# The feed-forward layernorm of a sequence's two halves, taken together in one PSUM bank

## The chip, the cores and the metric

One core of a Trainium2 chip runs the whole kernel. The time is the device time of one execution in microseconds, and a kernel's time is the median of its runs.

The engines are named as in the profile: PE (TensorE matmuls), PEld (TensorE weight loads), DVE (VectorE), ACT (ScalarE), POOL (GpSimd), SP (SyncE, which issues most DMAs).

## The reference, cut to what matters

`x` is (32 sequences, 256 tokens, 256 features). A state-space block (projection, causal convolution of 4 taps, layernorm, a scan over the 256 tokens, gate, projection) gives the input of two transformer layers. The result is added to `x`. The change is in the second half of a layer, the feed-forward:

```python
def _layer(x, wqkv, qs, ksc, wo, lg, lb, w1, b1, w2, b2):
    ...                                  # attention; x = x + o @ wo
    h = shift_token(x)                   # the second 128 features come from the token before
    mu = h.mean(-1, keepdims=True)
    var = h.var(-1, keepdims=True)
    h = (h - mu) / jnp.sqrt(var + 1e-05) * lg + lb
    h = h @ w1 + b1                      # 256 -> 2 x 682
    a, g = jnp.split(h, 2, axis=-1)
    h = a * jax.nn.gelu(g, approximate=False)
    x = x + h @ w2 + b2
    return x
```

All data are float32.

## The kernel before, in words

**Layout.** The 32 sequences make 4 groups of 8. In the transformer a sequence's state is `res[b]`, features in the partitions (two blocks of 128, `KM`) and tokens along the row. [...] PE transposes a half of the sequence (`W` = 128 tokens, `NW` = 2 halves) into a PSUM bank, DVE takes mean and variance per token, POOL raises variance plus epsilon to the power -1/2, DVE normalises, PE transposes back, and ACT copies to `hT` with gain and bias.

**Two streams.** The scan of the state-space block is a chain of 1024 DVE steps (L703, `h`), each on a row that a DMA spreads over the partitions (`xrep`) and ACT scales (L693). The first group's scan runs alone. The scans of groups 2 to 4 run beside the attention and feed-forward of the group before, which are 64 passes in all (4 groups, 2 layers, 8 sequences). The last group's layers run alone.

**Order.** Work is written as stages: `stage(n, i, what)` puts a piece into slot `8 * n + i`, where `n` counts the 64 passes. A loop walks through the slots and advances the scan by two steps in each slot, so 16 scan steps go with one pass, and a chunk of the scan (32 steps) with two. Within that order a scheduler may shift instructions of one engine against another engine's when the program is built, so an engine's final order isn't quite that of the slots. Instructions in `keep_in_program_order` keep their place on their engine. [...]

**PSUM.** All of it is one pool, `ps_w`, of 8 banks of 128 x 512 float32 under one tag. Each `bank(...)` takes a bank that was given back, in turn, so a new tile usually waits for the last reader of the tile of some seven allocations before.

**Pieces around the change**, with slots counted from the pass's slot 0 of the feed-forward:

- `Attention.sums` (slot 7 of the pass before): the softmax sums, then `rinv` on DVE (L1195). `values`: `ov` in two banks, each copied by ACT to oT (L1213).
- `turn` (slot 0, and slot 6): 8 transposes `tr_qk` (L1001) of a rotated query and key, copied by ACT to qT and kT (L1006).
- `project` (slots 0, 1, 1 and 3, 4, 4): `project_qkv` makes value, query and key of a half in one bank each (`ps_qkv`, L962); `rotated` reads query and key with ACT (`sq`, L975) and DVE (`rot` L978, `swp` L983), then POOL (L986, L994, L995).
- `FeedForward.normalise(w)` (slots 0 and 1 for the halves 0 and 1): two transposes `tp_h` (L1248), `st` (L1252), `mv` (L1254), `ve` (L1256), the power `rstd` (L1258). `apply(w)` (slots 1 and 2): `hn` (L1265). `spread(w)` (slots 2 and 3): two transposes `tp_hn` (L1278) and two ACT copies to `hT` (L1280).
- `scores` (slots 2, 3, 5): `sc` in two banks each, mask and products (L1161, L1168), exponentials to pT (L1177).
- `widen(m)` (slots 4 to 9): `pa` (L1301), the gelu of its half on ACT (`ag`, L1309). `product(m)` (a slot later): DVE multiplies into `ag` (L1317), which frees the bank of `pa`. The sixth chunk has only 42 rows (682 = 5 x 128 + 42) and is multiplied twice. So the last `widen` and `product` of one pass lie beside the layernorm of the next.
- `narrow(d)` (slots 3 and 4 of the next pass): `po_f` (L1329), added to `res` or `fo` by DVE (L1340).

Of the kernel before, what the change touches and what calls it, by code (L numbers as in the profile page):

```python
# [10 lines left out]
FP = mybir.dt.float32  # L11
# [3 lines left out]
ALU = mybir.AluOpType  # L15
# [4 lines left out]
P = 128  # L20
S = 256
DM = 256
KM = DM // P
# [15 lines left out]
W = 128  # L39
NW = S // W  # L40
# [3 lines left out]
LN_EPS = 1e-5  # L44
# [29 lines left out]
def kernel(  # L74
# [29 lines left out]
    nc = tc.nc  # L104
# [40 lines left out]
    ident = const.tile([P, P], FP, tag="ident", name="ident")  # L145
# [24 lines left out]
    neg_half = const.tile([P, HEADS], FP, tag="neg_half", name="neg_half")  # L170
# [43 lines left out]
    for i in range(2):  # L214
        t = const.tile([P, NI * (P + GB)], FP, tag=f"ly{i}", name=f"ly{i}")
# [3 lines left out]
    def program(ctx, exact):  # L219
# [7 lines left out]
        ap_ = ctx.enter_context(tc.tile_pool(name="at", bufs=2, reuse_waits="tile"))  # L227
        aw = ctx.enter_context(tc.tile_pool(name="aw", bufs=3, reuse_waits="tile"))
        ps_w = ctx.enter_context(tc.tile_pool(name="psw", bufs=8, space=PSUM, reuse_waits="tile"))

        def bank(pool, tag, name):
            return pool.tile([P, DI], FP, tag=tag, name=name)
# [681 lines left out]
        def scan_slots(groups):  # L914


            slots, scans = {}, [group_scan(g) for g in groups]
            for part in range(2):
                for i, agendas in enumerate(scans):
                    for s, what in agendas[part].items():  # L920
                        slots.setdefault(i * S + s, []).extend(what)
            for s in range(min(slots), max(slots) + 1):
                for what in slots.get(s, ()):
                    what()
                yield s


        ys, res, wt, projected = {}, {}, {}, {}

        def load_res(g, b):  # L930
            t = rpool.tile([P, KM, 1 + S], FP, tag=f"res{b}", name=f"res{b}")
            nc.gpsimd.memset(t[:, :, 0:1], 0.0)
            nc.sync.dma_start(out=t[:, :, 1:], in_=ys[g][:, :, b, :])
            res[b] = t

        def load_weights(l, kind, i=0):
            shape, srcs = {
                "qkv": lambda: ([P, KM, DI], [wqkv[:, l, :, i * DI : (i + 1) * DI]]),
                "wo": lambda: ([P, NC_, DM], [wo[:, l]]),
                "w1": lambda: (  # L940
                    [P, KM, 2, MCH[i][1]],
                    [w1[:, l, :, x * HID + MCH[i][0] :][:, :, 0 : MCH[i][1]] for x in range(2)],
                ),
                "w2": lambda: ([P, len(MCH), DM], [w2[:, l]]),
            }[kind]()
            t = wpool.tile(shape, FP, tag=f"{kind}{i}", name=f"{kind}{i}")
            for x, src in enumerate(srcs):
                nc.sync.dma_start(out=t[:, :, x] if len(srcs) > 1 else t, in_=src)
            if kind == "w2":
                last = len(MCH) - 1  # L950
                nc.sync.dma_start(out=t[DH : DH + MREM, last], in_=w2[0:MREM, l, last])
            wt[kind, i] = t
# [174 lines left out]
        class Attention:  # L1127
# [3 lines left out]
            def __init__(self, l):  # L1131
                self.l = l
                self.qkv, self.rot, self.p, self.o = {}, {}, {}, {}
# [102 lines left out]
        class FeedForward:  # L1236
# [2 lines left out]

            def __init__(self, g, l, b):  # L1240
                self.g, self.l, self.b = g, l, b
                self.hn, self.pa, self.ag = {}, {}, {}

            def normalise(self, w):
                tp = bank(ps_w, "w", "tp_h")
                for k in range(KM):
                    t0 = 1 - k + w * W
                    nc.tensor.transpose(  # L1248
                        tp[:, k * P : (k + 1) * P], res[self.b][:, k, t0 : t0 + W], ident
                    )  # L1250
                st = aw.tile([P, 6], FP, tag="st", name="st")
                nc.vector.bn_stats(st, tp[:, 0:DM])  # L1252
                mv = aw.tile([P, 2], FP, tag="mv", name="mv")
                nc.vector.bn_aggr(mv, st)  # L1254
                ve = aw.tile([P, 1], FP, tag="ve", name="ve")
                nc.vector.tensor_scalar_add(ve, mv[:, 1:2], LN_EPS)  # L1256
                rstd = aw.tile([P, 1], FP, tag="rstd", name="rstd")
                nc.gpsimd.tensor_tensor(rstd, ve, neg_half[:, 0:1], ALU.pow)  # L1258
                self.hn[w] = tp, mv, rstd

            def apply(self, w):
                tp, mv, rstd = self.hn[w]
                hn = ap_.tile([P, DM], FP, tag="hn", name="hn")
                tc.keep_in_program_order(
                    nc.vector.tensor_scalar(  # L1265
                        hn, tp[:, 0:DM], mv[:, 0:1], rstd, ALU.subtract, ALU.mult
                    )
                )
                self.hn[w] = hn

            def spread(self, w):
                if w == 0:
                    self.h = ap_.tile([P, KM, S], FP, tag="hT", name="hT", bufs=1)
                hn = self.hn.pop(w)
                tp = bank(ps_w, "w", "tp_hn")
                for k in range(KM):
                    ks = slice(k * P, (k + 1) * P)
                    nc.tensor.transpose(tp[:, ks], hn[:, ks], ident)  # L1278
                for k in range(KM):
                    nc.scalar.activation(  # L1280
                        self.h[:, k, w * W : (w + 1) * W],
                        tp[:, k * P : (k + 1) * P],
                        AF.Identity,
                        bias=flb_sb[:, self.l, k : k + 1],
                        scale=flg_sb[:, self.l, k : k + 1],
                    )
# [65 lines left out]
        if exact:  # L1352
            for g in range(NG):
                for _ in scan_slots([g]):
                    pass
                for b in range(GB):
                    load_res(g, b)
                for l in range(L):
                    for kind, i in WEIGHTS:
                        load_weights(l, kind, i)  # L1360
                    for _ in attention(l):
                        pass
                    for b in range(GB):
                        ff = FeedForward(g, l, b)
                        for w in range(NW):
                            ff.normalise(w)
                            ff.apply(w)
                            ff.spread(w)
                        for m in range(NM):
                            ff.widen(m)  # L1370
                            ff.product(m)
                        for d in range(KM):
                            ff.narrow(d)
            return
# [8 lines left out]
        def stage(n, i, what, *args):  # L1383
            stages.setdefault(ST * n + i, []).append(partial(what, *args))
# [18 lines left out]

        def feed(n, g, l, b):
            ff = FeedForward(g, l, b)
            for w in range(NW):
                stage(n + 1, 8 + w, ff.normalise, w)
                stage(n + 2, 1 + w, ff.apply, w)
                stage(n + 2, 2 + w, ff.spread, w)
            for m in range(NM):  # L1410
                stage(n + 2, 4 + m, ff.widen, m)
                stage(n + 2, 5 + m, ff.product, m)
            for d in range(KM):
                stage(n + 3, 3 + d, ff.narrow, d)
# [16 lines left out]
        for n, (g, l, b) in enumerate(seqs):  # L1431
            nxt = (ats[n + 1], seqs[n + 1][2]) if n + 1 < len(seqs) else None
            attend(n, ats[n], b, nxt)
            feed(n, g, l, b)
# [39 lines left out]
    with tc.If(fits > 0) as which:  # L1474
        with ExitStack() as es:
            program(es, False)
    with which.Else():
        with ExitStack() as es:
            program(es, True)
# [108 lines left out]
```

## Time and profile before

| | us |
|---|---|
| median of 3 runs (3755.57 to 3771.47) | 3759.6 |
| the profiled execution: its time | 3750.8 |
| the profiled execution: its span | 3748.7 |
| 600 to 2850 us, layers and scans together: PE busy, of 2250 | 2186.0 |
| 2850 to 3750 us, layers alone: PE busy, of 900 | 887.9 |

| instruction of the layernorm | count | mean ns |
|---|---|---|
| `st`, DVE L1252 | 128 | 427 |
| `mv`, DVE L1254 | 128 | 176 |
| `ve`, DVE L1256 | 128 | 149 |
| `rstd`, POOL L1258 | 128 | 646 |
| `hn`, DVE L1265 | 128 | 542 |
| `hT`, ACT L1280 | 256 | 453 |

The profile is of one execution. [...] The times in the waits view are those in which the waiting engine stood still; what released it is inferred. [...]

### The profile page before, as it was taken

The page shows a single profiled execution, that of the slowest core. Times are in us where ns is not written, and L with a number is a line of the kernel's source. Part 1 is how long each engine was busy: PE and PEld are TensorE (multiplying, and loading weights), DVE is VectorE, ACT ScalarE, POOL GpSimd, SP SyncE. Part 2 cuts the span into 40 slices and gives each one's busy share as a digit, 9 for nine tenths or more (in the row PEclk, how much of TensorE's full clock was granted, in tenths as well). Part 3 has the DMA queues.
Part 4 walks back from the last instruction along what each step waited for, and adds up shares of the span by engine and source line. Part 5 has one row for each costly group of instructions (what it writes and reads, how often), then busy time and mean ns, then how long its engine had stood idle before and what let it go on. Part 6 is the DMA issues. An engine that isn't in the chain of part 4 may idle for free.

```text
span 3748.7 us, 57254 instructions
## 1 busy us (share of the span) xinstructions
PE 3601.1 (96%) x19900; PEld 2242.4 (60%) x19900; DVE 2669.6 (71%) x5177; ACT 2195.4 (59%) x3817; POOL 1834.9 (49%) x1776
## 2 busy tenths in 40 slices
PE   7999889999999999999999999999999999999998
PEld 4444335656656665665666665656666666666666
DVE  6888889888787787778777877777777444444443
ACT  4666656666666666666666665666666444444442
POOL 4433466545555565455455555645444444434441
PEclk9999999999999999999999999999999999999999
DMA  7777655445454545434444545444443211011101
GB/s 210 205 198 202 189 163 149 120 117 135 127 137 129 147 123 146 120 112 122 120 128 116 147 124 147 121 108 126 112 129 103 57 40 50 12 34 34 30 25 35
DMA packets 469214, 435.81 MB, mean 116 GB/s; under 512 B 228835, under 2 KB 308532, under 8 KB 468788
## 3 DMA queue, kind: packets, MB, share of 16 engines
q1 hardware_dynamic: 384466, 420.05, 40.1%
q10 hardware_dynamic: 84450, 12.01, 2.0%
q8 instruction: 160, 2.62, 0.3%
q14 instruction: 138, 1.13, 0.1%
HBM read 383.70 MB, written 46.66 MB: 115 GB/s over the span
## 4 chain that ended last, share of the span: by engine, by line
PE 62%; DVE 16%; POOL 7%; ACT 6%; DMA 5%; issue 3%; SPq 0%; ACTq 0%; DVEq 0%; POOLq 0%
PE ps_qkv L962 12%; PE pa L1301 12%; PE po_f L1329 7%; DVE h L703 6%; PE y L715 4%; PE ps_wo L1012 4%; DMA xrep<-xnd 4%; PE sc L1168 4%; PE ov L1206 3%; PE ps_out L793 2%; ACT xrep L693 2%; DVE acc L485 2%; PE tr_qk L1001 2%; PE ps_in L395 2%; POOL acc L474 2%
## 5 line engine op out<-in xcount | busy, mean ns | idle before, releaser
L703 DVE CUSTOM_DVE_ANT_0 h<-h,xrep,lim 128x512 f32<-128x512 f32 x1024 | 948.2, 926 | 269.2 <-ACT xrep L693 238.8
L693 ACT ACTIVATE xrep<-xrep,beta 128x512 f32<-128x512 f32 x960 | 674.1, 719 | 333.0 <-DMA xrep<-xnd 235.9
L962 PE MATMUL ps_qkv<-qkv,res 128*128 128x512 f32 x1536 | 727.1, 610 | 45.2 <-DVE ag L1317 30.1
L1301 PE MATMUL pa<-hT,w 128*128 128x256 f32 (+1 forms) x3072 | 688.3, 386 | 0.3 <-ACT oT L1213 0.3
L1301 PEld LDWEIGHTS pa<-hT,w 128*128 128x128 f32 (+1 forms) x3072 | 492.9, 178 | 183.7 <-issue 66.5
L962 PEld LDWEIGHTS ps_qkv<-qkv,res 128*128 128x128 f32 x1536 | 282.4, 194 | 335.4 <-issue 263.3
L986 POOL TENSOR_TENSOR rot<-rot,swp 128x512 f32<-128x512 f32 x256 | 336.5, 1314 | 293.0 <-DVE swp L983 239.2
L1258 POOL TENSOR_TENSOR rstd<-ve,neg_half 128x1 f32<-128x1 f32 x128 | 82.7, 646 | 792.9 <-DVE ve L1256 787.8
L994 POOL TENSOR_TENSOR rn<-ss,neg_half 128x8 f32<-128x8 f32 x256 | 460.3, 1798 | 14.8 <-DVE ss L992 5.0
L1329 PE MATMUL po_f<-ag,w 128*128 128x256 f32 (+1 forms) x1536 | 387.8, 394 | 4.8 <-DVE res L1340 1.1
L715 PE MATMUL y<-h,ly 128*32 128x512 f32 x2048 | 354.9, 612 | 12.9 <-DVE h L703 11.7
L1329 PEld LDWEIGHTS po_f<-ag,w 128*128 128x128 f32 (+1 forms) x1536 | 273.6, 190 | 112.9 <-issue 44.6
L1317 DVE SCALAR_TENSOR_TENSOR ag<-pa,b_sb,ag 128x256 f32<-128x256 f32 (+1 forms) x448 | 212.4, 474 | 166.5 <-ACT ag L1309 163.0
L975 ACT ACTIVATE sq<-ps_qkv 128x512 f32<-128x512 f32 x256 | 152.1, 596 | 270.5 <-PE ps_qkv L962 234.6
L995 POOL TENSOR_TENSOR rot<-rot,rn 128x512 f32<-128x512 f32 x256 | 298.6, 1166 | 20.1
L1309 ACT ACTIVATE ag<-pa,b_sb 128x256 f32<-128x256 f32 x320 | 150.4, 470 | 198.5 <-PE pa L1301 197.4
L1012 PE MATMUL ps_wo<-oT,wo 128*128 128x256 f32 x1024 | 231.6, 379 | 0.0
L485 DVE SCALAR_TENSOR_TENSOR acc<-xr,wc_sb,acc 128x256 f32<-128x256 f32 x384 | 192.7, 525 | 52.9 <-POOL acc L474 52.6
L1177 ACT ACTIVATE pT<-sc 128x512 f32<-128x512 f32 x384 | 208.5, 596 | 32.2 <-PE sc L1168 30.7
L1168 PE MATMUL sc<-qT,kT 64*128 64x128 f32 (+1 forms) x2048 | 221.5, 345 | 0.0
L978 DVE TENSOR_TENSOR rot<-ps_qkv,rc_sb 128x512 f32<-128x512 f32 x256 | 175.0, 683 | 56.5 <-ACT sq L975 55.9
L1012 PEld LDWEIGHTS ps_wo<-oT,wo 128*128 128x128 f32 x1024 | 194.5, 190 | 27.2 <-PE y L715 0.8
(150 smaller groups left out, 5534.7 us busy)
## 6 DMA issues: line engine op xcount, KB each, us to landing
xrep<-xnd SPq DMA_DIRECT2D x960, 256.0 KB
rb<-inv SPq DMA_DIRECT2D x128, 256.0 KB
xnd<-xn SPq DMA_DIRECT2D x64, 256.0 KB
qkv<-in_wqkv_dram SPq DMA_DIRECT2D x24, 512.0 KB
ahead<-xs_a SPq DMA_DIRECT2D x48, 256.0 KB
xp<-ahead SPq DMA_DIRECT2D x48, 256.0 KB
xd<-xnd SPq DMA_DIRECT2D x192, 64.0 KB
w<-in_w_dram SPq DMA_DIRECT2D x80, 128.0 KB
```

What stands on the lines that cost most here:

```text
L485: nc.vector.scalar_tensor_tensor(acc, xr[:, :, k : k + CH], wc_sb[:, ch, k : k + 1], acc, ALU.mult, ALU.add,)
L693: scaled = nc.scalar.activation(bx, ck[c].pop(("bx", t), bx), AF.Copy, scale=ck[c]["beta"][:, t : t + 1])
L703: nc.vector._custom_dve(TENSOR_ADD_SAT, out=h_new, in0=state["h"], in1=bx, s0=ck[c]["lim"][:, 0, t : t + 1], s1=ck[c]["lim"][:, 1, t : t + 1],
L715: nc.tensor.matmul(ck[c]["y", hb][32 * q : 32 * q + 32, :], ly[hb % 2][:, 32 * t : 32 * t + 32], ck[c].pop(("h", hb * TB + t)), start=(i = ...
L962: nc.tensor.matmul(ps, res[b][:, k, t0 : t0 + W], wt["qkv", a][:, k], start=(k == 0), stop=(k == KM - 1),)
L986: nc.gpsimd.tensor_add(rot, rot, swp)
L994: nc.gpsimd.tensor_tensor(rn, ss, neg_half, ALU.pow)
L995: nc.gpsimd.tensor_mul(rot, rot, bc(rn, 2, DH))
L1012: nc.tensor.matmul(po[:, d], wt["wo", 0][:, c, d * P : (d + 1) * P], oT[:, c, :], start=(c == 0), stop=(c == NC_ - 1),)
L1168: nc.tensor.matmul(banks[r][:, i, :], kT[rows, i0 + i, kw * W : (kw + 1) * W], qT[rows, i0 + i, kw * W :], start=False, stop=(i == n - 1),)
L1301: nc.tensor.matmul(pg if x else pa, wt["w1", m][:, k, x], self.h[:, k], start=(k == 0), stop=(k == KM - 1),)
L1329: nc.tensor.matmul(self.po[:, d], wt["w2", 0][r0 : r0 + n, m, d * P : (d + 1) * P], self.ag[m][r0 : r0 + n], start=(m == 0), stop=(m == le ...
```

## The change

The two halves of a sequence go through the layernorm together. `normalise` puts all four transposes in one bank, takes two `st` and two `mv`, and then one `ve` and one power of two columns. `apply` makes both `hn` one after the other into one buffer. `spread` transposes all four blocks into one bank, ordered by feature block, so that two copies of 256 columns fill `hT` where there were four of 128. The slots are now 0, 1 and 3.

```diff
-            def normalise(self, w):
-                tp = bank(ps_w, "w", "tp_h")
-                for k in range(KM):
-                    t0 = 1 - k + w * W
-                    nc.tensor.transpose(
-                        tp[:, k * P : (k + 1) * P], res[self.b][:, k, t0 : t0 + W], ident
-                    )
-                st = aw.tile([P, 6], FP, tag="st", name="st")
-                nc.vector.bn_stats(st, tp[:, 0:DM])
...
-                ve = aw.tile([P, 1], FP, tag="ve", name="ve")
-                nc.vector.tensor_scalar_add(ve, mv[:, 1:2], LN_EPS)
-                rstd = aw.tile([P, 1], FP, tag="rstd", name="rstd")
-                nc.gpsimd.tensor_tensor(rstd, ve, neg_half[:, 0:1], ALU.pow)
+            def normalise(self):
+                tp = bank(ps_w, "w", "tp_h").rearrange("p (w n) -> p w n", w=NW)
+                for w in range(NW):
+                    for k in range(KM):
+                        t0 = 1 - k + w * W
+                        nc.tensor.transpose(
+                            tp[:, w, k * P : (k + 1) * P],
+                            res[self.b][:, k, t0 : t0 + W],
+                            ident,
+                        )
+                mv = aw.tile([P, NW, 2], FP, tag="mv", name="mv")
+                for w in range(NW):
+                    st = aw.tile([P, 6], FP, tag="st", name="st")
+                    nc.vector.bn_stats(st, tp[:, w])
+                    nc.vector.bn_aggr(mv[:, w], st)
+                ve = aw.tile([P, NW], FP, tag="ve", name="ve")
+                nc.vector.tensor_scalar_add(ve, mv[:, :, 1], LN_EPS)
+                rstd = aw.tile([P, NW], FP, tag="rstd", name="rstd")
+                nc.gpsimd.tensor_tensor(rstd, ve, neg_half[:, 0:NW], ALU.pow)
...
-            def apply(self, w):
...
-                hn = ap_.tile([P, DM], FP, tag="hn", name="hn")
+            def apply(self):
...
+                hn = ap_.tile([P, NW, DM], FP, tag="hn", name="hn", bufs=1)
+                for w in range(NW):
+                    tc.keep_in_program_order(
+                        nc.vector.tensor_scalar(
+                            hn[:, w], tp[:, w], mv[:, w, 0:1], rstd[:, w : w + 1],
+                            ALU.subtract, ALU.mult,
+                        )
+                    )
...
-            def spread(self, w):
...
-                tp = bank(ps_w, "w", "tp_hn")
-                for k in range(KM):
-                    ks = slice(k * P, (k + 1) * P)
-                    nc.tensor.transpose(tp[:, ks], hn[:, ks], ident)
+            def spread(self):
+                self.h = ap_.tile([P, KM, S], FP, tag="hT", name="hT", bufs=1)
+                tp = bank(ps_w, "w", "tp_hn").rearrange("p (k t) -> p k t", k=KM)
+                for w in range(NW):
+                    for k in range(KM):
+                        nc.tensor.transpose(
+                            tp[:, k, w * W : (w + 1) * W],
+                            self.hn[:, w, k * P : (k + 1) * P],
+                            ident,
+                        )
                 for k in range(KM):
                     nc.scalar.activation(
-                        self.h[:, k, w * W : (w + 1) * W],
-                        tp[:, k * P : (k + 1) * P],
+                        self.h[:, k],
+                        tp[:, k],
                         AF.Identity,
                         bias=flb_sb[:, self.l, k : k + 1],
                         scale=flg_sb[:, self.l, k : k + 1],
...
         def feed(n, g, l, b):
             ff = FeedForward(g, l, b)
-            for w in range(NW):
-                stage(n + 1, 8 + w, ff.normalise, w)
-                stage(n + 2, 1 + w, ff.apply, w)
-                stage(n + 2, 2 + w, ff.spread, w)
+            stage(n + 2, 0, ff.normalise)
+            stage(n + 2, 1, ff.apply)
+            stage(n + 2, 3, ff.spread)
             for m in range(NM):
                 stage(n + 2, 4 + m, ff.widen, m)
                 stage(n + 2, 5 + m, ff.product, m)
```

More of the change, by code (lines that the diff above doesn't have):

```diff
@@ L1241, in __init__ @@
                 self.g, self.l, self.b = g, l, b
-                self.hn, self.pa, self.ag = {}, {}, {}
-            def normalise(self, w):
-                tp = bank(ps_w, "w", "tp_h")
-                for k in range(KM):
-                    t0 = 1 - k + w * W
-                    nc.tensor.transpose(
-                        tp[:, k * P : (k + 1) * P], res[self.b][:, k, t0 : t0 + W], ident
-                    )
-                st = aw.tile([P, 6], FP, tag="st", name="st")
-                nc.vector.bn_stats(st, tp[:, 0:DM])
-                mv = aw.tile([P, 2], FP, tag="mv", name="mv")
-                nc.vector.bn_aggr(mv, st)
-                ve = aw.tile([P, 1], FP, tag="ve", name="ve")
-                nc.vector.tensor_scalar_add(ve, mv[:, 1:2], LN_EPS)
-                rstd = aw.tile([P, 1], FP, tag="rstd", name="rstd")
-                nc.gpsimd.tensor_tensor(rstd, ve, neg_half[:, 0:1], ALU.pow)
-                self.hn[w] = tp, mv, rstd
@@ L1261, in apply @@
-            def apply(self, w):
-                tp, mv, rstd = self.hn[w]
-                hn = ap_.tile([P, DM], FP, tag="hn", name="hn")
-                tc.keep_in_program_order(
-                    nc.vector.tensor_scalar(
-                        hn, tp[:, 0:DM], mv[:, 0:1], rstd, ALU.subtract, ALU.mult
-                    )
-                )
-                self.hn[w] = hn
-            def spread(self, w):
-                if w == 0:
-                    self.h = ap_.tile([P, KM, S], FP, tag="hT", name="hT", bufs=1)
-                hn = self.hn.pop(w)
-                tp = bank(ps_w, "w", "tp_hn")
-                for k in range(KM):
-                    ks = slice(k * P, (k + 1) * P)
-                    nc.tensor.transpose(tp[:, ks], hn[:, ks], ident)
+                self.pa, self.ag = {}, {}
@@ new lines, in normalise @@
+            def normalise(self):
[17 more added lines that the diff above has]
+                nc.gpsimd.tensor_tensor(rstd, ve, neg_half[:, 0:NW], ALU.pow)
+                self.hn = tp, mv, rstd
@@ new lines, in apply @@
+            def apply(self):
+                tp, mv, rstd = self.hn
+                hn = ap_.tile([P, NW, DM], FP, tag="hn", name="hn", bufs=1)
[5 more added lines that the diff above has]
+                        )
+                    )
+                self.hn = hn
+            def spread(self):
[8 more added lines that the diff above has]
+                        )
@@ L1364, in program @@
                         ff = FeedForward(g, l, b)
-                        for w in range(NW):
-                            ff.normalise(w)
-                            ff.apply(w)
-                            ff.spread(w)
+                        ff.normalise()
+                        ff.apply()
+                        ff.spread()
                         for m in range(NM):
@@ L1405, in feed @@
             ff = FeedForward(g, l, b)
-            for w in range(NW):
-                stage(n + 1, 8 + w, ff.normalise, w)
-                stage(n + 2, 1 + w, ff.apply, w)
-                stage(n + 2, 2 + w, ff.spread, w)
+            stage(n + 2, 0, ff.normalise)
+            stage(n + 2, 1, ff.apply)
+            stage(n + 2, 3, ff.spread)
             for m in range(NM):
```

## The prediction

> **What bounds the kernel now.** I read the page first: who is busy, and what the chain that ended last is made of.
>
> ```profile
> PE 3601.1 (96%) x19900; PEld 2242.4 (60%) x19900; DVE 2669.6 (71%) x5177; ACT 2195.4 (59%) x3817; POOL 1834.9 (49%) x1776
> ...
> PE 62%; DVE 16%; POOL 7%; ACT 6%; DMA 5%; issue 3%; SPq 0%; ACTq 0%; DVEq 0%; POOLq 0%
> ```
>
> TensorE is nearly full, so only its gaps can be won; but over a third of the chain is not on TensorE. The windows view says where. The layernorm first runs at 600 us. From 600 to 2850 us PE is busy 2186.0 of 2250 us, so 64 us are gaps; from 2850 to 3675 us it is gapless, one sequence in every 41.6 us, and nothing can be won there. Before 600 us there is no feed-forward. So I asked for PE's waits between 600 and 2850 us (waiter, releaser: us in all, times, longest):
>
> ```profile
> PE ps_qkv L962 <- DVE ag L1317: 30.1, 13, 2.7
> PE ps_qkv L962 <- DVE rinv L1195: 7.2, 14, 0.9
> PE sc L1161 <- DVE ag L1317: 5.8, 7, 1.0
> PE tp_hn L1278 <- DVE hn L1265: 4.1, 2, 3.5
> ```
>
> Half of the gaps is one wait: a query/key projection wants a PSUM bank that a `product` (`ag`, L1317) still holds. It comes once in two sequences, 12 times of 2.2 to 2.7 us. Both timelines around one of them (start, length, engine, line; idle before, releaser):
>
> ```profile
> 2384.11 0.38 PE L1248 MATMUL tp_h<-ident,res 128*128 128x128 f32 x2
> 2384.33 1.04 PE L1001 MATMUL tr_qk<-ident,rot 128*128 128x128 f32 x8
> 2385.57 1.98 PE L962 MATMUL ps_qkv<-qkv,res 128*128 128x512 f32 x4 [0.21 <-DVE rinv L1195]
> 2387.49 1.07 PE L1301 MATMUL pa<-hT,w 128*42 128x256 f32 x8
> 2388.49 0.44 PE L1248 MATMUL tp_h<-ident,res 128*128 128x128 f32 x2
> 2391.33 5.40 PE L962 MATMUL ps_qkv<-qkv,res 128*128 128x512 f32 x8 [2.41 <-DVE ag L1317]
> ```
>
> ```profile
> 2388.76 0.81 DVE L703 CUSTOM_DVE_ANT_0 h<-h,xrep,lim 128x512 f32<-128x512 f32 x1 [3.24 <-ACT xrep L693]
> 2389.74 0.81 DVE L703 CUSTOM_DVE_ANT_0 h<-h,xrep,lim 128x512 f32<-128x512 f32 x1 [0.17 <-DVE h L703]
> 2390.47 0.43 DVE L1252 BATCH_NORM_STATS2 st<-tp_h 128x6 f32<-128x256 f32 x1
> 2390.81 0.47 DVE L1317 SCALAR_TENSOR_TENSOR ag<-pa,b_sb,ag 128x256 f32<-128x256 f32 x1
> ```
>
> DVE is late (a scan row came late by DMA), works off two scan steps and a layernorm statistic, and only then the `ag` at 2390.81. PE has stood since 2388.92. Two more things are seen. The second `tp_h` takes a bank just before the projections: with 8 banks in turn it pushes the first projection onto the bank of the youngest `pa`. And the projections after the wait last 5.40 us instead of 3.70: in 7 of the 12 cases (5.2 to 5.4).
>
> Followed back, the chain from such a wait leaves PE in the sequence before, and passes through the layernorm itself:
>
> ```profile
> 2339.37 0.49 DVE ag L1317
> 2339.86 0.02 issue
> 2339.88 0.17 DVE ve L1256
> 2340.04 0.07 issue
> 2340.11 0.56 POOL rstd L1258
> 2340.67 0.02 issue
> 2340.70 0.54 DVE hn L1265
> 2341.24 0.60 DVE rot L978
> ```
>
> The second half's `ve`, power and `hn` stand ahead of the rotation: 1.38 us of the path.
>
> [...] 2.4 us of waiting next to transposes is followed by 5.40 us for work of 3.70, in some cases and not in others. [...] POOL stands 787.8 us ahead of `rstd`, 121 times, with later work behind it. [...]
>
> **The change part by part**, per sequence, 64 sequences; the engines' orders are those of the changed build.
>
> *Removed.* One `ve` (149 ns) and one power (646 ns); two of four copies to hT. The copies now follow each other in 403 ns (103.1 us/256); a 128x256 copy isn't in the trace. Nearest row: `ag` 128x256 from PSUM with a bias, 470 ns[...]. I take 470: 1.61 - 0.94 = 0.67 us less ACT (0.5 to 0.7). ACT, POOL and DVE have idle time elsewhere, so none of this moves the end by itself. In the gapless part (22 sequences) it is worth 0: PE covers it.
>
> *Kept.* Eight transposes. Two in a row cost 0.22 us start to start (2384.11 to 2384.33), or 0.28 after the 42-row `pa`; that switch stays, now in front of `ps_qkv`. PE's own work: 0 (both ends under 0.1 us a sequence, 3 us in all). No DMA is added; SP's queue keeps its rows but for a few neighbours exchanged.
>
> *Bank order (the main term).* In the built order `tp_h` and `tp_hn` take one bank each instead of two. In the sequences with the wait, the first projection then gets the bank of `ov`, freed by the copy oT (ended 2388.11 here, before PE is free at 2388.5); only the second gets the bank of `ag`. So one projection, 3.43/2 = 1.72 us, slips in front of the wait. Besides, DVE's order becomes `ag, st, st, aggr, aggr, ve, hn, hn`: `ag` ahead of `st`, 0.34 us earlier (2390.47 to 2390.81). The wait shrinks from 2.48 (mean) to 2.48 - 1.72 + 0.28 (the `tp_h` pair gone from there) - 0.34 = 0.70 us, and the second projection ends 1.72 + 0.34 = 2.06 us earlier: 12 x 2.06 = **24.7 us**. Bounds: 1.4 if `ag` isn't earlier and the four transposes hold `st` up by 0.28; 2.7 if the wait goes altogether: 17 to 32.
>
> *Clock.* With 0.7 us of idle instead of 2.5, the half-rate stretches should go: 7 x 1.7 = **11.9 us** (0 to 12[...]).
>
> *The layernorm on the chain.* In the other sequences the built order is `ve, hn, hn, sg, ag(42), ag(42), rot`: after the first 42-row `ag` only the second stands, 0.40 us, and the rotation begins at about 2340.4 instead of 2341.16: 0.75 us earlier on the path to the next `rinv` and `ag`. It shortens what is left of the waits on `rinv`, `sc` and `ag`: 12 x 0.75 = **9 us** (0 to 12).
>
> *Early sequences (600 to 1300 us).* `tp_hn` moves to slot 3, so PE no longer meets `hn` too early (3.51, 0.61 and 1.49 us): **5 us** (-3 to 8, since the DVE order there changes more irregularly).
>
> *Added waits.* The second `hn` now stands ahead of the 42-row `ag` and the rotations. In the waiting sequences two scan steps also come ahead of them, so `rot` starts about 0.7 us later. Behind it wait POOL's rotation and later `tr_qk`, over 15 us later in the trace, and `sc` through the bank of `swp` (about 2397.3, PE there at 2398.7): covered, if narrowly. Spread in one piece: PE reaches `tp_hn` about 4 us after `hn` is done; hT is read by `pa` some 10 us later. The bank of `tp_h` is held until both `hn`; its next user `po_f` comes about 3 us later. 0 each.
>
> *Sum.* 24.7 + 11.9 + 9 + 5 = 50.6 us. A ceiling checks it: between 1420.17 and 2711.01 us a pair of sequences takes 107.6 us, and PE's own work in one is 99.9 (2396.73 to 2497.40) + 3.4 = 103.3, so 12 pairs can give at most 51; my three terms give 45.6. As PE gets nearer to its ceiling, waits come back elsewhere; I take off 6: **45 us**. The profiled execution took 3750.8 us (span 3748.7), so 3705.8; it lies 8.8 us under the median of 3759.6. On the median: **3715**.
>
> **Rivals.**
> 1. *The gap moves.* PE comes 2 us earlier to the next thing that DVE holds (`rinv`, `sc`), and the pair's length is set by DVE, ACT and the DMA of scan rows, not by PE. For: 38% of the chain lies off PE, with DMA and `xrep` in it. Against: the layernorm part of that chain gets shorter too. Then only the 0.75 and some clock remain: 5 to 18 us, 3742 to 3755.
> 2. *Slower.* In all 44 sequences of the scan stretch DVE's later work is pushed back: `rot` by 0.7 us, or, in the other sequences, `ag` behind two `st` and one `aggr`, 0.34 + 0.2 = 0.54 us. If the rotation's way through POOL (1.3 + 1.7 + 1.2 us twice) into `sc` or `tr_qk` decides, or PE's second projection waits for that `ag`, 0.54 to 0.7 x 44 = 24 to 31 us are lost: 3784 to 3791. It decides only once PE is over 1.4 us (`sc`) or 4 us (`ag`: ends about 2335.4, wanted about 2340) earlier than DVE. PE does get earlier by about 2, which speaks for it; the order holds no second such wait, which speaks against.
> 3. *All gaps go*, the 64 us and the slow clock: 3684.
> That the change does not do what it says is excluded by the built order: one power, two copies, two banks fewer.
>
> **How the numbers follow.** Half a per cent, 19 us, is about what a measurement of this kernel can tell from no change. My case (25 to 65 us won) has 0.62, rival 3 0.06, rival 1 0.20, rival 2 0.12. Faster by over 19 us: 0.62 + 0.06 + a little of rival 1 = 0.70; within: 0.18; slower: 0.12. The range runs from 3682 (nearly every gap gone) to 3770 (rival 1 and the mild end of rival 2); my case alone would be 3695 to 3735.
>
> **What would show it.** Right: PE's wait for `ag` at `ps_qkv` falls from 30 us to under 10, no `ps_qkv` pair of 5.4 us, the pair of sequences takes about 104 us instead of 107.6, the part after the scan keeps 41.6 us a sequence, hT copies near 470 ns. Wrong: waits on `rinv` or `sc` that have grown by as much, `ps_qkv` at half rate after them, or a pair no shorter than 107 us.

## The result, and the profile after

The changed kernel takes **3716.1 us** (median, 3714.0 to 3719.8) beside 3760.1 us for the kernel before (3755.6 to 3771.5, run on the same chip): ratio 0.9883, 95% interval 0.9867 to 0.9899. The forecast was 3715. Its profiled execution has a span of 3714.5 us.

The first part of the page of after, and its chain of waits by engine:

```profile
PE 3594.4 (97%) x19900; PEld 2240.4 (60%) x19900; DVE 2671.9 (72%) x5113; ACT 2161.5 (58%) x3689; POOL 1775.9 (48%) x1712
...
PE 66%; DVE 15%; DMA 6%; POOL 5%; ACT 4%; issue 3%; SPq 0%; ACTq 0%; DVEq 0%; POOLq 0%
```

The same matmuls were 6.7 us shorter on PE (3601.1 before), and PE's share of the chain rose from 62 to 66%, while POOL's fell from 7 to 5. PE's waits in the same stretch as before, 600 to 2850 us (waiter, releaser: us in all, times, longest):

```profile
PE ps_qkv L962 <- DVE ag L1325: 8.1, 12, 0.9
PE po_f L1337 <- DVE ag L1325: 7.7, 3, 5.3
PE sc L1161 <- DVE ag L1325: 4.5, 7, 0.9
PE po_f L1337 <- DVE fo L1348: 3.3, 1, 3.3
PE ps_qkv L962 <- DVE rinv L1195: 2.4, 5, 0.8
```

The 30.1 us of projections waiting for `ag` became 8.1: still 12 times, but 0.68 us each. The waits of `po_f` for DVE have grown: 11.0 us, where before had 2.6; after's lie in the early passes alone. One waiting pass on PE and then on DVE (start, length; idle before, releaser; the page counts 1536 of L962 for the program's 768 matmuls, so its x4 are two matmuls, one projection):

```profile
2363.39 0.60 PE L1249 MATMUL tp_h<-ident,res 128*128 128x128 f32 x4
2363.82 1.04 PE L1001 MATMUL tr_qk<-ident,rot 128*128 128x128 f32 x8
2364.86 1.98 PE L962 MATMUL ps_qkv<-qkv,res 128*128 128x512 f32 x4
2366.77 1.06 PE L1309 MATMUL pa<-hT,w 128*42 128x256 f32 x8
2367.77 1.98 PE L962 MATMUL ps_qkv<-qkv,res 128*128 128x512 f32 x4
2370.36 1.99 PE L962 MATMUL ps_qkv<-qkv,res 128*128 128x512 f32 x4 [0.60 <-DVE ag L1325]
```

```profile
2368.12 0.81 DVE L703 CUSTOM_DVE_ANT_0 h<-h,xrep,lim 128x512 f32<-128x512 f32 x1 [3.31 <-ACT xrep L693]
2369.09 0.81 DVE L703 CUSTOM_DVE_ANT_0 h<-h,xrep,lim 128x512 f32<-128x512 f32 x1 [0.17 <-DVE h L703]
2369.82 0.48 DVE L1325 SCALAR_TENSOR_TENSOR ag<-pa,b_sb,ag 128x256 f32<-128x256 f32 x1
2370.22 0.75 DVE L1257 BATCH_NORM_STATS2 st<-tp_h 128x6 f32<-128x256 f32 x2
```

DVE is as late as before: the scan row still comes late, and DVE waits 3.31 us for it. But one projection (2367.77) now fits into PE's wait, `ag` is ahead of `st`, and the second projection takes 1.99 us, its normal length. In the pass before, the layernorm is gone from the chain that leads here; ACT's `sq` hands over directly to the rotation (start, length, piece):

```profile
2317.42 1.93 PE ps_qkv L962 x4
2319.35 0.02 issue
2319.38 0.61 ACT sq L975
2319.98 0.02 issue
2320.00 0.69 DVE rot L978
```

**The accounts.** The output projection `ps_wo` of a pass marks its place in every trace. Each kernel was also traced a second time. The parts of the span in us:

| from ... to | before | again | after | again |
|---|---|---|---|---|
| start to pass 1 | 584.6 | 600.5 | 589.5 | 590.1 |
| pass 1 to 5 | 216.3 | 216.8 | 212.6 | 213.2 |
| pass 5 to 14 | 488.7 | 494.7 | 499.1 | 500.1 |
| pass 14 to 40 ("the middle") | 1403.8 | 1405.1 | 1361.0 | 1361.6 |
| pass 40 to the end | 1055.3 | 1055.3 | 1052.4 | 1052.4 |

Of the 34.2 us between the first two spans (3748.7 and 3714.5), the middle gave 42.8 and the end 2.9; the passes up to the 14th took 6.6 back, and the start, which the layernorm has no part in and which scatters by 16 us, 4.9. The first traced execution of before was a quick one (3750.8 us, with a median of 3760.1), so these 34.2 us are less than the 44.0 us between the medians. The second pair of spans differs by 54.9 us (3772.4 and 3717.5), and there too the middle gives 43.4 and the end 2.9. The windows view for the middle, of before and of after (length; busy time of PE, PEld, DVE, ACT, POOL; granted clock):

```profile
1289.62:2693.38 1403.76, 1358.32 (x7801) 857.76 (x7800) 1086.57 (x2094) 880.45 (x1538) 753.14 (x701) 0.99 0.45 125
1301.17:2662.14 1360.97, 1345.64 (x7802) 852.60 (x7801) 1085.29 (x2066) 867.41 (x1486) 718.06 (x674) 1.00 0.48 128
```

PE's busy time fell by 12.7 us for the same matmuls, and its waits, summed over the waits view of the same windows, from 45.2 to 14.7, by 30.5. Together 43.2, beside the 42.8 us by which the middle is shorter. These two explain it, so the experiments below are compared there first.

### The profile page after: what moved, and what is told of

Its sections match the earlier page's. It is cut to its first block, busy times and chain, and to the rows that moved or that the text cites. A ratio compares the mean times of both kernels' runs of the same rounds, so it can differ in the third digit from the quotient of the medians.

```text
span 3714.5 us, 56989 instructions
## 1 busy us (share of the span) xinstructions
PE 3594.4 (97%) x19900; PEld 2240.4 (60%) x19900; DVE 2671.9 (72%) x5113; ACT 2161.5 (58%) x3689; POOL 1775.9 (48%) x1712
## 4 chain that ended last, share of the span: by engine, by line
PE 66%; DVE 15%; DMA 6%; POOL 5%; ACT 4%; issue 3%; SPq 0%; ACTq 0%; DVEq 0%; POOLq 0%
PE ps_qkv L962 13%; PE pa L1309 13%; PE po_f L1337 8%; DVE h L703 6%; PE y L715 5%; PE ps_wo L1012 4%; DMA xrep<-xnd 4%; PE sc L1168 4%; PE ov L1206 3%; PE ps_out L793 2%; PE ps_in L395 2%; PE tr_qk L1001 2%; ACT xrep L693 2%; DVE acc L485 2%; PE rs L1187 2%
## 5 line engine op out<-in xcount | busy, mean ns | idle before, releaser
L962 PE MATMUL ps_qkv<-qkv,res 128*128 128x512 f32 x1536 | 724.4, 607 | 18.4 <-DVE ag L1325 8.1
L962 PEld LDWEIGHTS ps_qkv<-qkv,res 128*128 128x128 f32 x1536 | 277.8, 191 | 327.9 <-issue 251.1
L994 POOL TENSOR_TENSOR rn<-ss,neg_half 128x8 f32<-128x8 f32 x256 | 459.2, 1794 | 15.2 <-DVE ss L992 5.2
L1337 PE MATMUL po_f<-ag,w 128*128 128x256 f32 (+1 forms) x1536 | 386.9, 393 | 11.6 <-DVE ag L1325 7.7
L1262 POOL TENSOR_TENSOR rstd<-ve,neg_half 128x2 f32<-128x2 f32 x64 | 46.3, 723 | 622.3 <-DVE ve L1260 604.0
```

The source lines that it names most:

```text
L962: nc.tensor.matmul(ps, res[b][:, k, t0 : t0 + W], wt["qkv", a][:, k], start=(k == 0), stop=(k == KM - 1),)
L994: nc.gpsimd.tensor_tensor(rn, ss, neg_half, ALU.pow)
L1337: nc.tensor.matmul(self.po[:, d], wt["w2", 0][r0 : r0 + n, m, d * P : (d + 1) * P], self.ag[m][r0 : r0 + n], start=(m == 0), stop=(m == le ...
```

## The experiments

Each ratio is to runs of the kernel before on the same chip, where its median was 3760.1 to 3764.2 us, so two kernels are better compared by their ratios and by the middle than by their times. Three theories. **1, bank order:** what counts is which bank each projection meets, that is, which tile had it before (its tenant), and so where the layernorm takes its banks. **2, DVE's order:** the gain comes from `ag` ahead of the statistics, and the layernorm out of the path to the rotation. **3, fewer operations:** it comes from the power, the `ve` and the two copies that are gone. The middle in all kernels (us):

| kernel | middle | PE waits | PE busy | time | ratio to before, 95% |
|---|---|---|---|---|---|
| before | 1403.8 | 45.2 | 1358.3 | 3760.1 | 1 |
| after | 1361.0 | 14.7 | 1345.6 | 3716.1 | 0.9883 (0.9867 to 0.9899) |
| all_ops | 1361.5 | 14.7 | 1345.6 | 3718.5 | 0.9876 (0.9852 to 0.9900) |
| early_product | 1362.6 | 16.4 | 1345.6 | 3715.5 | 0.9882 (0.9864 to 0.9900) |
| two_tp_h | 1370.5 | 21.9 | 1346.6 | 3723.5 | 0.9906 (0.9890 to 0.9923) |
| slots_only | 1374.3 | 23.2 | 1348.0 | 3724.7 | 0.9886 (0.9862 to 0.9910) |
| two_tp_hn | 1379.1 | 28.4 | 1349.8 | 3731.2 | 0.9927 (0.9910 to 0.9944) |
| slots_123 | 1389.0 | 38.5 | 1350.2 | 3743.4 | 0.9949 (0.9931 to 0.9968) |
| filler | 1393.8 | 24.9 | 1368.6 | 3754.9 | 0.9982 (0.9973 to 0.9991) |
| late_second | 1417.2 | 52.2 | 1364.3 | 3778.9 | 1.0043 (1.0033 to 1.0054) |
| one_tp_h | 1443.5 | 70.8 | 1371.9 | 3808.0 | 1.0109 (1.0085 to 1.0134) |
| slots_223 | 1511.8 | 123.9 | 1387.8 | 4076.4 | 1.0831 (1.0805 to 1.0857) |

### Operations back, banks and slots kept (all_ops)

```diff
-                ve = aw.tile([P, NW], FP, tag="ve", name="ve")
...
-                nc.gpsimd.tensor_tensor(rstd, ve, neg_half[:, 0:NW], ALU.pow)
+                for w in range(NW):
+                    ve = aw.tile([P, 1], FP, tag="ve", name="ve")
+                    nc.vector.tensor_scalar_add(ve, mv[:, w, 1:2], LN_EPS)
+                    nc.gpsimd.tensor_tensor(
+                        rstd[:, w : w + 1], ve, neg_half[:, 0:1], ALU.pow
+                    )
...
+                for w in range(NW):
                     for k in range(KM):
                         nc.scalar.activation(
-                            self.h[:, k],
-                            tp[:, k],
+                            self.h[:, k, w * W : (w + 1) * W],
+                            tp[:, k, w * W : (w + 1) * W],
```

> The changed kernel with its banks and slots, but two ve, two powers and four copies of 128 columns again. Theories 1 and 2: at most 5 us lost, 3714 to 3722, since ACT, POOL and DVE have room for them. Theory 3 (fewer operations make the gain): back to 3750 to 3760.

3718.5 us, and in the middle 1361.5 beside 1361.0, with the same waits. The one power, the one `ve` and the two copies are worth nothing that can be measured. Theory 3 falls.

### Slots alone (slots_only)

```diff
             for w in range(NW):
-                stage(n + 1, 8 + w, ff.normalise, w)
-                stage(n + 2, 1 + w, ff.apply, w)
-                stage(n + 2, 2 + w, ff.spread, w)
+                stage(n + 2, 0, ff.normalise, w)
+            for w in range(NW):
+                stage(n + 2, 1, ff.apply, w)
+            for w in range(NW):
+                stage(n + 2, 3, ff.spread, w)
```

> The kernel before, with the slots of after and nothing else: both normalise(w) in slot 0, both apply(w) in slot 1, both spread(w) in slot 3; two banks of each kind, two ve, two powers, four copies. Both tp_h banks are now taken ahead of the value projection, so the first query/key projection no longer meets ag. Theory 1: it is where a bank is taken that counts and not how many, so most of the gain is there: 3720 to 3735. If the number of banks counts by itself: 3745 to 3760. Theory 3 (fewer operations): no change, 3755 to 3760.

Nothing is merged here, not even a bank, and 29.5 of the 42.8 us of the middle are won (1403.8 to 1374.3). Both `tp_h` banks are now taken ahead of the value projection; no projection waits for `ag` any more. It is the place in the order and not the number of banks that matters most. The rest, 13.3 us, lies in small waits; one waiting pass on PE:

```profile
2368.72 0.60 PE L1248 MATMUL tp_h<-ident,res 128*128 128x128 f32 x4
2369.16 0.60 PE L1001 MATMUL tr_qk<-ident,rot 128*128 128x128 f32 x4
2370.28 0.63 PE L1001 MATMUL tr_qk<-ident,rot 128*128 128x128 f32 x4 [0.52 <-DVE rinv L1195]
2370.74 1.88 PE L962 MATMUL ps_qkv<-qkv,res 128*128 128x512 f32 x4
2373.21 1.06 PE L1301 MATMUL pa<-hT,w 128*42 128x256 f32 x8 [0.59 <-ACT oT L1213]
2374.67 4.09 PE L962 MATMUL ps_qkv<-qkv,res 128*128 128x512 f32 x8 [0.40 <-ACT qT L1006]
```

The second `tp_h` bank pushes everything behind it one bank on, to tenants that are freed later: `rinv`, oT, qT.

### The place undone, the merging kept (late_second)

```diff
-            stage(n + 2, 0, ff.normalise)
+            for w in range(NW):
+                stage(n + 2, w, ff.normalise, w)
...
-            def normalise(self):
-                tp = bank(ps_w, "w", "tp_h").rearrange("p (w n) -> p w n", w=NW)
+            def normalise(self, w):
+                tp = bank(ps_w, "w", "tp_h")
...
+                if w == 0:
+                    return
                 ve = aw.tile([P, NW], FP, tag="ve", name="ve")
```

> The changed kernel, with the order of banks undone: the second half's tp_h has a bank of its own again, taken in slot 1 as before, between the value projection and the query/key projections; one ve, one power, one tp_hn bank, two copies stay, and both hn follow the power. Theory 1 (bank order): the wait of ps_qkv for ag is back in every second sequence at 2 us or more, with projections of 5.4 us: 3745 to 3760. Theory 2 (DVE's order) and theory 3 (fewer operations): 3716 to 3725, for the merged ve, power and copies are all there.

It is slower than the kernel before. One power, one `tp_hn` bank and two copies are all there; the waits of the middle are back (first lines of its waits view, 600 to 2850 us):

```profile
PE ps_qkv L962 <- DVE ag L1325: 33.4, 14, 2.7
PE sc L1161 <- DVE ag L1325: 12.3, 13, 1.5
```

The first line is the wait of before, at 2.4 us each. The second has doubled from 5.8 us. Rival 2 of the prediction priced something of this kind: both `hn` ahead of the rotations delay `rot`, and with it the next `ag` and `sc`. That this is the way was not shown apart. Merging without the place costs 13.4 us of the middle.

### The bank shared, the slots kept (one_tp_h)

```diff
-                tp = bank(ps_w, "w", "tp_h")
+                if w == 0:
+                    self.tp = bank(ps_w, "w", "tp_h").rearrange("p (w n) -> p w n", w=NW)
+                tp = self.tp[:, w]
```

> The kernel before, with one edit: both halves' tp_h share one bank, taken in slot 0; two ve, two powers, two tp_hn banks, four copies, and the slots of before stay. Theory 1 (bank order): in every second sequence the first query/key projection now meets oT instead of ag, the wait of 2.4 us falls under 1 us, and the long projections of 5.4 us go with it: 25 to 37 us won, 3723 to 3735 us. Theory 2 (the order of DVE's layernorm, ve and hn off the path to the rotation): only the part of it that comes with fewer banks, so at most 10 us, about 3750. Theory 3 (fewer operations): no change, 3755 to 3760.

All theories missed: 1.1% slower. The order of banks is that of after, but the bank is now written, read and written again (one waiting pass on PE):

```profile
2323.53 1.06 PE L1303 MATMUL pa<-hT,w 128*42 128x256 f32 x8
2328.66 0.69 PE L1250 MATMUL tp_h<-ident,res 128*128 128x128 f32 x2 [4.07 <-DVE hn L1267]
2329.14 4.75 PE L962 MATMUL ps_qkv<-qkv,res 128*128 128x512 f32 x8
```

The second half's transposes wait until `hn` of the first half has read the shared bank, which comes after `st`, `mv`, `ve` and POOL's power. The two halves touch different columns of it; the wait is there all the same. Whether the program's order or the chip asks for it, no run shows. Sharing paid only with all four transposes ahead of the first reader, which is what after's `normalise` does.

### One bank more, of either kind (two_tp_h, two_tp_hn)

```diff
-                tp = bank(ps_w, "w", "tp_h").rearrange("p (w n) -> p w n", w=NW)
+                tp = [bank(ps_w, "w", "tp_h") for _ in range(NW)]
```

> The changed kernel with one bank more: tp_h takes one bank for each half, both in slot 0; one power, one tp_hn bank, two copies, and the slots of after. slots_only (3724.7 us) lacked 8 us of after's gain. If that is the second tp_h bank, which pushes tr_qk onto the bank of rs (rinv) and the projections onto kT and qT: about 3725, with tr_qk waiting for rinv some 8 us. If it is the second tp_hn bank or the operations: 3716 to 3719.

As expected: 3723.5 us, and 9.5 us more in the middle than after, with `tr_qk` waiting 7.3 us for `rinv`. That is most of what slots_only lacked.

This run is also the counterpart of late_second: the same merging and the same two banks, but the second half's `tp_h` in slot 0 and not in slot 1, and its statistics with it. The middle takes 1370.5 us beside 1417.2, and no projection waits for `ag`. So the place alone is worth 46.7 us between these two.

```diff
-                tp = bank(ps_w, "w", "tp_hn").rearrange("p (k t) -> p k t", k=KM)
+                tp = [bank(ps_w, "w", "tp_hn") for _ in range(KM)]
```

> The changed kernel with one bank more: tp_hn takes one bank for each block of features; all else is after's. It is taken past the first three projections, so they meet the same banks as in after. If the single tp_h bank carries what merging adds to the slots: 3714 to 3720. If the tp_hn bank carries it: about 3725.

A miss. The first three projections do meet the same banks, but the tiles behind `tp_hn` are pushed on as well, to banks that DVE holds (two lines of its waits view, 600 to 2850 us):

```profile
PE sc L1161 <- DVE swp L983: 8.5, 13, 1.8
PE ps_qkv L962 <- DVE xd L764: 6.8, 13, 0.5
```

18.1 us of the middle are lost to one bank. Together with a second `tp_h` bank, as in slots_only, it costs less (13.3), presumably because the two shifts together lead to another position in the ring of eight; that was not followed up. One bank more cost 9.5 us in one place and 18.1 in the other; the question is who had it before.

### Is it the idling that slows PE? (filler)

```diff
+            def keep(self, again=False):
+                b, w, ps = self.v
+                if again:
+                    project_qkv(b, w, 2, ps)
+                nc.scalar.copy(self.qkv[b][2][:, w], ps)
...
+                        hold = n % 2 == 1 and 13 < n < 46 and w == 0
+                        if hold and a == 0:
+                            stage(n, 1, nxt[0].keep, True)
```

> The kernel before, with work put into the wait: in every second sequence of the scan stretch (16 of them) the first half's value projection is computed a second time into its own bank, two matmuls of 1.98 us in all, directly ahead of the query/key projections that wait 2.4 us for ag; its copy v_sb follows it. If idling is what makes the projections after the wait take 5.40 us instead of 3.70: the wait shrinks to about 0.5 us, its seven long pairs become 3.70 us, and some 10 us are won by work that is thrown away: 3748 to 3755 beside 3760. If the long pairs have another cause (transposes ahead, the bank): they stay, and the time stays at 3760 or goes up by as much as 16 x 0.5 = 8 us through the later v_sb.

The waiting pass on PE:

```profile
2391.23 0.44 PE L1257 MATMUL tp_h<-ident,res 128*128 128x128 f32 x2
2391.50 1.88 PE L963 MATMUL ps_qkv<-qkv,res 128*128 128x512 f32 x4
2394.34 3.70 PE L963 MATMUL ps_qkv<-qkv,res 128*128 128x512 f32 x8 [0.95 <-DVE ag L1326]
```

The projection at 2391.50 is computed for nothing. The pair behind it takes 3.70 us, and so does each of the others: no long pair is left in the middle. It is won back with thrown-away work: 9.9 us in the middle, 6.3 us of time (three of the 16 repeats fall behind pass 40, and the end is 4.8 us longer). The bank and its tenant are the same as before, and the transposes still stand ahead, if not directly. So filling the idle time takes the long pairs away.

The traces themselves record how: they hold the times at which the granted clock of TensorE changed. Three stretches of before around its pair at 2391.33 (windows view: length; busy time of PE, PEld, DVE, ACT, POOL; granted clock, DMA share, GB/s):

```profile
2389.02:2392.43 3.41, 1.10 (x3) 0.62 (x4) 2.51 (x7) 2.61 (x6) 0.58 (x1) 1.00 0.46 151
2392.43:2395.84 3.41, 3.41 (x6) 1.35 (x5) 3.35 (x8) 0.60 (x1) 1.06 (x1) 0.50 0.75 190
2395.84:2399.25 3.41, 3.41 (x28) 1.38 (x29) 3.22 (x9) 2.42 (x5) 2.49 (x3) 1.00 0.30 106
```

For 3.41 us, from 1.1 us into the pair, the clock is at half. That costs half of 3.41, 1.7 us, which is what 5.40 has over 3.70. The middle of before has seven such stretches, one at each long pair; the middle of filler has none, nor has that of after. In the traces of before and of after the changes of the clock (48 and 32) lie on a grid of 3.41 us, within 1 ns over the whole trace, so it matters where in the grid a wait falls. In the two traces of before, the next step of the grid was at half where 2.04 us or more of a wait lay inside one step (14 waits), and at full clock where it was 1.93 us or less (9 waits). The limit isn't quite sharp: in late_second two waits with 1.67 and 1.87 us inside a step were followed by half, others up to 1.72 were not.

### Later slots (slots_123, slots_223)

```diff
-            stage(n + 2, 0, ff.normalise)
-            stage(n + 2, 1, ff.apply)
+            stage(n + 2, 1, ff.normalise)
+            stage(n + 2, 2, ff.apply)
```

> The changed kernel with everything of the layernorm but its end one slot later: normalise in slot 1, apply in slot 2, spread in slot 3. tp_h's bank is then taken behind the value projection. If only the place of the bank counts: the value projection meets the bank that tp_h had, the query/key projections the same ones as after, so 3712 to 3722. If the layernorm must be early (hn behind the rotations on DVE, hT then late for pa): PE waits for hn or hT, 3730 to 3770.

> The changed kernel with normalise and apply in slot 2 and spread in slot 3: tp_h's bank is taken behind all three projections of the first half, so each of them meets a bank that was taken one place earlier, and none waits for the youngest ag: the 8.1 us of ps_qkv for ag go, 3703 to 3714. If the layernorm must be early: 3730 to 3770, with waits of PE at tp_hn for hn or at pa for hT.

(slots_223 has 2 for both.) Neither is better. In slots_123 the banks are as good, but `ag` is not: in the middle `sc` waits 13.9 us and `po_f` 11.6 us for it. In slots_223 `hn` itself is too late, as its waits view (600 to 2850 us) has it:

```profile
PE tp_hn L1282 <- DVE hn L1270: 174.1, 37, 11.1
```

A good bank is worth nothing if the layernorm's result is late. Slot 0 is early enough for both.

### The last `ag` ahead of the statistics (early_product)

```diff
-                stage(n + 2, 5 + m, ff.product, m)
+                stage(n + 2, 4 + m if m == NM - 2 else 5 + m, ff.product, m)
```

> The changed kernel with the product of the fifth chunk (the last ag of 128 rows) one slot earlier, so that DVE's order has it ahead of st and mv in every sequence and not only in every second; nothing is left out. If the place of this ag against the statistics costs PE something (the prediction's 0.34 to 0.54 us a sequence): the waits of sc and ov for ag shrink and the time falls by up to 5 us, 3710 to 3716. If the late scan row and ACT's gelu set it: 3716, within 3 us. Slower, 3720 to 3730, if the early sequences, where DVE's order shifts most, lose more.

1362.6 us in the middle beside 1361.0, the time the same. DVE's order of `ag` and `st`, in the passes where after has it the other way round, costs nothing that can be measured in the middle.

### How far one trace can be trusted (before_again, after_again)

No edit: the two kernels once more.

> The kernel before a second time, for its trace: how far one execution's stretches scatter. From the 5th to the 14th pass (ps_wo at 800.9 and 1289.6 us, 488.7 us) the first trace of after took 10.4 us longer. If that is the change: 489 us again here, within 2. If it is scatter: 492 us or more. From the 14th to the 40th pass: 1403.8 us again within 3, with the same waits of 2.4 us and about seven pairs of 5.4 us.

> The changed kernel a second time, for the same: if the loss in the early passes belongs to the change, 499 us from the 5th to the 14th pass within 2; if it is scatter, 490 to 496 us. From the 14th to the 40th pass 1361.0 us again within 3.

The middle and the end repeat within 1.3 us (table of the accounts), and so do seven long pairs of 5.35 to 5.40 us. From pass 5 to 14 before scatters by 6.0 us, after by 1.0; the loss of the change there is 4.4 to 11.4 us, not 10.4. Most of it lies in one place: between the marks of passes 8 and 9, before takes 49.3 and 50.0 us and after 56.4 and 55.5.

## Why the prediction was right

**Bank order, 24.7 us: right.** The wait was to fall to 0.70 us and is 0.68; the waits for `ag` at `ps_qkv` gave 22.0 us (30.1 to 8.1). late_second, with the place undone, has them back, two_tp_h with the same two banks in the earlier place has none, and slots_only wins 29.5 us of the middle by the place. What I had put down to fewer banks is mostly the place; the number adds 13.3 us, by pushing later tiles less far.

**Clock, 11.9 us: right.** PE's busy time in the middle fell by 12.7 us; the seven long pairs had 11.7 us over 3.70 each. The recorded clock and filler show the cause: seven stretches at half clock in before and none in after, and with the wait filled, and the bank the same, the pairs are normal. What sets these seven of twelve waits apart is where they fell in the grid: 2.04 to 2.36 us of each lay inside one step, and at most 1.74 us of the other five. That 0.7 us of waiting would leave the clock at full was my estimate; in the middle of after it did.

**The layernorm on the chain, 9 us: the size is right, the way is argued.** The waits other than that for `ag` at `ps_qkv` fell by 30.5 - 22.0 = 8.5 us: `rinv` from 6.6 to 2.0, `sc` from 4.9 to 3.6, `ov` from 1.6 to nothing. The chain now passes from `sq` to `rot`. But two_tp_h and two_tp_hn show that a bank's position makes and removes waits of this size too, and no run separates the two.

**Early passes, +5 us: this step failed.** The wait for `hn` that was to go, 3.5 us, went: pass 1 to 5 is 3.6 to 3.8 us shorter in each pair of traces. But from pass 5 to 14 the change loses 4.4 to 11.4 us, and over passes 1 to 14 the two pairs of traces lose 6.6 and 1.8, where I had a gain of 5 and a loss of 3 as the bound. Between the marks of passes 8 and 9, PE and DVE of after:

```profile
1000.40 1.22 PE L1337 MATMUL po_f<-ag,w 42*128 42x256 f32 x2 [5.25 <-DVE ag L1325]
```

```profile
995.50 0.76 DVE L983 TENSOR_TENSOR swp<-ps_qkv,rs_sb 128x256 f32<-128x256 f32 x2 [1.23 <-POOL rot L986]
...
998.13 1.82 DVE L703 CUSTOM_DVE_ANT_0 h<-h,xrep,lim 128x512 f32<-128x512 f32 x1
999.88 0.47 DVE L1325 SCALAR_TENSOR_TENSOR ag<-pa,b_sb,ag 42x256 f32<-42x256 f32 x1
```

The wait, 5.33 us in the second trace, is short at the same place in before (0.84 us in its second trace):

```profile
994.71 0.70 PE L1329 MATMUL po_f<-ag,w 42*128 42x256 f32 x2 [0.22 <-DVE ag L1317]
```

In after the second 42-row `ag` stands last on DVE, behind two rotations and a scan step, and PE comes to it earlier. The wait comes with the slots: slots_only, with nothing merged, has it with 3.24 us, and all_ops with 3.21. early_product, which moves one `ag` earlier on DVE and changes nothing else, has 2.15 there. From pass 5 to 14 these three take 495.3, 492.2 and 495.9 us, less than after; but each has one trace, and before scatters by 6 us, so what the merged operations and DVE's order add there stays open. I had read only the waits for `hn` in these passes and not asked what DVE does next; "DVE order there changes more irregularly" was the place to look.

**What I left at nothing.** Operations: right (all_ops). A copy to hT of 256 columns: the line of ACT in the groups of after,

```profile
L1288 ACT ACTIVATE hT<-tp_hn,flb_sb,flg_sb 128x256 f32<-128x256 f32 x128 | 65.2, 562 | 69.0 <-PE tp_hn L1282 69.0
```

has 562 ns (and 65.2 us for 128 of them, 509 each, so they overlap a little): my nearest row (470) was wrong. ACT is off the path, so it cost nothing. The gapless part: 41.6 us a pass as forecast, but the last passes, which I had priced at 0, give 2.9 us in both pairs of traces; before, PE waited there twice 1.2 us at `tp_hn`.

**The sum.** My three terms of the middle made 45.6 us against 42.8 measured, and a pair of passes 104.7 us (1361.0/13) against "about 104". The 6 us taken off for returning waits were too many for the middle and stood in for the early loss, which I had with the wrong sign. Middle, end and early passes together give 39.1 us in the first pair of traces and 44.5 in the second, beside the 44.0 of the medians and my 45. So the mechanism of the middle was right, and the closeness of 3715 to 3716.1 is partly luck.

**The rivals.** Rival 1 (the gap moves): the waits on `rinv` and `sc` shrank. Rival 2 (slower): not in after; late_second has it. Rival 3 (all gaps go): 14.7 us of waits stay in the middle.

## What to carry to other kernels

Where tiles take banks from a ring, follow each tile to the tenant before it: moving an allocation past one projection was worth more here than all operations saved, and the wrong place made the same merged code slower than before. Sharing a tile between two halves paid only with both written before either was read. When a wait is removed, look at the same engine's next late result at that spot, in every stretch of the kernel, before booking the gain.

## What the runs showed of the hardware

Work that is thrown away can pay: filler adds 16 projections and is 6.3 us faster. In before, waits of 2.2 to 2.7 us, directly behind a pair of transposes, made seven of twelve pairs of projections 5.2 to 5.4 us instead of 3.70; in its second trace, waits of 2.0 to 2.7 us made it seven of eleven. The length of the wait does not separate the two kinds (2.36 us: long; 2.73 us: normal). How much of it falls into one step of the clock's grid of 3.41 us does: 2.04 us and more, long; up to 1.93 us, normal. So some 2 us of waiting within one step were enough for the half clock in the next. With at most 1.0 us of idle, behind 1.88 us of matmuls, as in filler, no pair of the middle was long; with waits of 3.2 to 4.8 us, as in one_tp_h, all thirteen were, with 4.7 to 6.4 us.

A power of two columns on POOL takes 723 ns in after (mean of 64) where one column took 646 in before (mean of 128), and `rn`, a power of eight columns, 1794 in after (mean of 256): the second column adds 77 ns, the next six some 180 each (the profile has spans on POOL only roughly).
